# Attention transposes moved ahead of the second FF matmul, the small FF groups moved by one cycle, and the first image's bias additions and the second image's norm chain moved

**Chip, cores, metric.** One core of one Trainium2 chip. The metric is device time in microseconds, as the median of several executions; all executions told here are in the fast state. A ratio is the mean time of one kernel's fast runs over the mean time of the other's fast runs of the same rounds, so it is not quite the ratio of the medians quoted beside it. The experiments ran on three chips; each ratio is against the kernel before on the same chip.

## The reference, cut to what matters

Two residual layers on an NHWC tensor of 32 images, 56 x 56 pixels, 128 channels, float32:

```python
x = x + window_attention(group_norm(x))       # 7x7 windows shifted by 3, 4 heads, relative bias, mask
x = x + feed_forward(fourier(group_norm(x)))  # 128 -> 512 -> relu -> 128

def fourier(x):   # once along the width, once along the height, summed
    modes = dct(x, norm='ortho')[..., :32]
    mixed = einsum('bixy,ioy->boxy', modes, w)
    return idct(pad_to_56(mixed), norm='ortho')
```

## The kernel before

The kernel is a software pipeline over rows of windows (8 rows an image, 256 in all), one "cycle" a row. In a cycle, TensorE works for several rows and images at once: q and k of this row, scores, v, values (attention times v) and projection of the row before the last, and the Fourier and feed-forward (FF) work of the two images before. The order on the four compute engines is set by hand; the transfers that SyncE issues (SP in the traces) are not in that set, and the toolchain places them. In the traces PE is TensorE, DVE VectorE, ACT ScalarE, POOL GpSimd. An eviction is the copy of a finished matmul result out of the accumulator bank that TensorE wrote it to.

```python
FF_GROUPS = (HB, HB, HB, HB, 320, 256, HB)   # HB = 512 tokens
FF_AT = (7, 8, 9, 10, 12, 13, 14)            # cycles of an image; none at 11
...
def full_first(cycle, norm):                 # full-array work, head of the cycle
    im, i = row(cycle - 2)
    if im:
        attn_transpose(im, i, cycle - 2)     # "aT": attention transposed for the values
    ...
    attn_qk(im, i, False)
    ... load_modes(im, width, g)             # "zT": mixed modes back from DRAM
    ... ff_in(im, FF_AT.index(c))
...                                          # half_columns, quarters (scores, modes_back), eighths (values)
def full_last(cycle, norm):                  # full-array work, tail of the cycle
    next(norm)
    if row(cycle - 2)[0]:
        last_out(cycle)                      # second FF matmul
    next_image(cycle)                        # 7 transposes of the next image
    if row(cycle)[0]:
        attn_exp(cycle)
    attn_project(im, j)                      # needs "oT", the evicted values
...
with tc.manual_schedule(engines={ET.PE, ET.Activation, ET.DVE, ET.Pool}):
```

## Time and profile before

| | us |
|---|---|
| time, median of 3 | 3668.28 (3667.28 to 3670.64) |
| span of the profiled run | 3669.3 |
| TensorE busy | 3603.8 (98%) |
| start: constants and first rows, to the first image's statistics | 106.1 |
| first image (no FF work yet) | 93.4 |
| 29 steady images | 3254.6, about 112 each |
| last but one image, and the end | 101.8 and 113.4 |

How to read it: an engine with 98% busy time can only be helped where it stands still or is started late, so the waits of TensorE (PE) are the list to work from. The prediction below shows the rows it used. It did not use one kind of row of the same list, those with the releaser "issue", which means that the profile shows nothing that PE was waiting for. Between 216 and 3540 us, these are three of the five largest rows of the kernel before (line, releaser, total, times, longest):

```profile
PE pc L633 <- issue: 3.8, 6, 1.0
...
PE pa L524 <- ACT oT L515: 1.0, 2, 0.7
PE pa L482 <- issue: 0.8, 2, 0.4
```

L633 is the Fourier transform, L482 the values: both are long runs of small matmuls. They matter later. (Line numbers move between kernels: in the changed kernel these two are L637 and L486.)

### The profile page before, as it was taken

The page shows a single profiled execution, that of the slowest core. Times are in us where ns is not written, and L with a number is a line of the kernel's source. Part 1 is how long each engine was busy: PE and PEld are TensorE (multiplying, and loading weights), DVE is VectorE, ACT ScalarE, POOL GpSimd, SP SyncE. Part 2 cuts the span into 40 slices and gives each one's busy share as a digit, 9 for nine tenths or more (in the row PEclk, how much of TensorE's full clock was granted, in tenths as well). Part 3 has the DMA queues.
Part 4 walks back from the last instruction along what each step waited for, and adds up shares of the span by engine and source line. Part 5 has one row for each costly group of instructions (what it writes and reads, how often), then busy time and mean ns, then how long its engine had stood idle before and what let it go on. Part 6 is the DMA issues. An engine that isn't in the chain of part 4 may idle for free.

```text
span 3669.3 us, 139900 instructions
## 1 busy us (share of the span) xinstructions
PE 3603.8 (98%) x61184; PEld 2938.0 (80%) x61184; DVE 2222.3 (61%) x4741; ACT 2152.8 (59%) x4043; POOL 1371.9 (37%) x1421
## 2 busy tenths in 40 slices
PE   7899999999999999999999999999999999999998
PEld 5687888888888888888888888878888888888786
DVE  7766666656666566666566665666656666656641
ACT  5565556655565656566555666565665565665653
POOL 5433334333334333343333343333343333433321
PEclk9999999999999999999999999999999999999999
DMA  4334443433433334334434334443344343443333
GB/s 116 97 102 111 107 109 93 118 106 102 115 97 106 108 106 113 105 98 118 106 101 117 97 108 107 109 111 99 103 110 110 102 115 98 111 108 106 96 108 90
DMA packets 687795, 388.93 MB, mean 106 GB/s; under 512 B 40495, under 2 KB 658128, under 8 KB 686928
## 3 DMA queue, kind: packets, MB, share of 16 engines
q1 hardware_dynamic: 686573, 379.65, 38.1%
q8 instruction: 482, 7.90, 0.9%
q14 instruction: 129, 1.06, 0.1%
q10 hardware_dynamic: 611, 0.32, 0.0%
HBM read 218.29 MB, written 161.48 MB: 103 GB/s over the span
## 4 chain that ended last, share of the span: by engine, by line
PE 91%; DVE 4%; ACT 2%; POOL 1%; issue 1%; DMA 0%; SPq 0%; POOLq 0%; DVEq 0%; ACTq 0%
PE pc L769 21%; PE pc L749 17%; PE pa L391 7%; PE pc L667 6%; PE pc L633 6%; PE pa L413 6%; PE pa L457 5%; PE pc L706 5%; PE pa L524 5%; PE pa L482 4%; PE pa L359 4%; PE pa L366 4%; PE pa L262 2%; POOL a L432 1%; DVE a L421 1%; DVE mx L431 1%
## 5 line engine op out<-in xcount | busy, mean ns | idle before, releaser
L769 PE MATMUL pc<-wff,hid 128*128 128x128 f32 (+1 forms) x6400 | 779.1, 279 | 1.0 <-ACT hid L757 0.9
L446 POOL TENSOR_TENSOR a<-a,rs 128x784 f32<-128x784 f32 x256 | 389.6, 1522 | 993.0 <-DVE rs L445 869.7
L769 PEld LDWEIGHTS pc<-wff,hid 128*128 128x128 f32 (+1 forms) x6400 | 731.1, 189 | 24.0 <-issue 2.9
L749 PE MATMUL pc<-xf,wff 128*128 128x512 f32 (+2 forms) x1792 | 710.9, 539 | 0.9 <-DVE xf L717 0.6
L757 ACT ACTIVATE hid<-pc,b1sb 128x512 f32<-128x512 f32 (+2 forms) x896 | 536.4, 635 | 93.0 <-PE pc L749 89.4
L749 PEld LDWEIGHTS pc<-xf,wff 128*128 128x128 f32 x1792 | 339.5, 190 | 310.3 <-issue 229.4
L432 POOL TENSOR_TENSOR a<-a,mx 128x784 f32<-128x784 f32 x256 | 388.8, 1519 | 456.9 <-DVE mx L431 448.0
L781 DVE TENSOR_TENSOR res<-pc,res 128x512 f32<-128x512 f32 (+3 forms) x259 | 144.1, 568 | 607.7 <-issue 293.9
L289 POOL TENSOR_TENSOR xl<-xl,bproj 112x512 f32<-112x512 f32 (+1 forms) x256 | 286.0, 1138 | 347.3 <-PE pa L262 338.8
L421 DVE TENSOR_TENSOR a<-pa,bm 128x392 f32<-128x392 f32 x512 | 259.7, 550 | 203.2 <-PE pa L413 203.1
L438 ACT ACTIVATE a<-a 128x784 f32<-128x784 f32 x256 | 225.0, 879 | 222.3 <-POOL a L432 221.9
L379 DVE TENSOR_SCALAR k<-pa,heads,bqkv 128x392 f32<-128x392 f32 x246 | 168.6, 685 | 288.0 <-ACT k L371 288.0
L465 ACT COPY aT<-pa 113x452 f32<-113x452 f32 x256 | 137.5, 537 | 303.0 <-PE pa L457 298.7
L398 ACT COPY v<-pa 128x512 f32<-128x512 f32 x256 | 152.5, 596 | 268.4 <-PE pa L391 268.3
L739 POOL TENSOR_TENSOR res<-res,b2sb 128x512 f32<-128x512 f32 (+2 forms) x256 | 263.7, 1035 | 98.5 <-DMA res<-scr 88.3
L413 PEld LDWEIGHTS pa<-k,q 64*64 64x64 f32 x8192 | 183.6, 132 | 137.7 <-DVE rs L445 67.5
L513 DVE TENSOR_SCALAR oT<-pa,bqkv 128x98 f32<-128x98 f32 (+2 forms) x768 | 170.6, 278 | 200.0 <-PE pa L482 200.0
L391 PE MATMUL pa<-wn,xw 128*64 128x128 f32 x4096 | 282.5, 280 | 5.4 <-DVE a L421 2.9
L391 PEld LDWEIGHTS pa<-wn,xw 128*64 128x64 f32 x4096 | 220.3, 137 | 55.5 <-issue 16.4
L524 PE MATMUL pa<-wproj,oT 128*112 128x128 f32 x1792 | 241.0, 274 | 12.6 <-DVE oT L513 7.2
L431 DVE TENSOR_REDUCE mx<-a 128x16 f32<-128x784 f32 x256 | 247.3, 966 | 5.5
L443 DVE TENSOR_REDUCE sm<-a 128x16 f32<-128x784 f32 x256 | 245.7, 960 | 5.0 <-ACT a L438 5.0
(91 smaller groups left out, 5899.7 us busy)
## 6 DMA issues: line engine op xcount, KB each, us to landing
zscr<-z SPq DMA_DIRECT2D x512, 112.0 KB
htok<-scr SPq DMA_DIRECT2D x256, 196.0 KB
zT<-zscr SPq DMA_DIRECT2D x192, 256.0 KB
res<-scr SPq DMA_DIRECT2D x160, 256.0 KB
out_dram<-res SPq DMA_DIRECT2D x128, 256.0 KB
scr<-xl SPq DMA_DIRECT2D x128, 224.0 KB
xl<-in_x_dram SPq DMA_DIRECT2D x32, 784.0 KB
xl<-in_x_dram SPq DMA_DIRECT2D x32, 672.0 KB
```

The lines of the kernel that those rows point to most:

```text
L289: nc.gpsimd.tensor_tensor(piece, piece, bproj.unsqueeze(1).to_broadcast([TC, e - a, C]), ALU.add)
L391: nc.tensor.matmul(pv[hs, j * C : (j + 1) * C], lhsT=im.xw[i][:, w * WT : w * WT + JP], rhs=im.w[:, 2 * C : 3 * C], start=True, stop=True,)
L413: nc.tensor.matmul(ps[hp][HALVES[e], pr * 2 * WT : (pr + 1) * 2 * WT], lhsT=q[cs, w * WT : w * WT + JP], rhs=k_sb[cs, :, w], start=True, s ...
L421: nc.vector.tensor_tensor(a[:, 2 * hp : 2 * hp + 2, :, 0:WT].rearrange("p u w j -> p w u j"), ps[hp][:, :RT].rearrange("p (w u j) -> p w u ...
L431: nc.vector.tensor_reduce(mx, a3, axis=AX.X, op=ALU.max)
L432: nc.gpsimd.tensor_tensor(a3, a3, mx.unsqueeze(2).to_broadcast([P, 2 * NWR, WT]), ALU.subtract)
L446: nc.gpsimd.tensor_tensor(a3, a3, rs.unsqueeze(2).to_broadcast([P, 2 * NWR, WT]), ALU.mult)
L524: nc.tensor.matmul(pp[:TC, (n - n0) * C : (n - n0 + 1) * C], lhsT=oT[:, (n - base) * TC : (n - base + 1) * TC], rhs=wproj, start=True, sto ...
L739: nc.gpsimd.tensor_tensor(res[:m, c0:c1], res[:m, c0:c1], b2sb[:m].unsqueeze(1).to_broadcast([m, c1 - c0, C]), ALU.add,)
L749: nc.tensor.matmul(ph[:, :n], lhsT=wff1[:, f * P : (f + 1) * P], rhs=xff[:, t0 : t0 + n], start=True, stop=True,)
L757: nc.scalar.activation(hf[:, :n], ph[:, :n], AF.Relu, bias=b1sb[:, f : f + 1])
L769: nc.tensor.matmul(pf[:m, c * C : (c + 1) * C], lhsT=im.hid[f][:, c * P : c * P + m], rhs=wff2[:, f], start=(f == 0), stop=(f == NF - 1),)
```

## The change

Its intent: the transposes of the attention for the values of the next cycle move from the head of a cycle to the tail of the one before, ahead of the second FF matmul and the projection, so that they are work that waits for nothing while the projection's input gets ready. The small FF groups move by one cycle. At the start, the bias additions leave the first image's norm chain, and the second image's norm chain moves behind the values.

```diff
-FF_GROUPS = (HB, HB, HB, HB, 320, 256, HB)
+FF_GROUPS = (HB, HB, HB, HB, HB, 320, 256)
...
 def full_first(cycle, norm):
-        im, i = row(cycle - 2)
-        if im:
-            attn_transpose(im, i, cycle - 2)
...
+    def transpose_next(cycle):
+        im, i = row(cycle - 1)
+        if im:
+            attn_transpose(im, i, cycle - 1)
...
     def full_last(cycle, norm):
+        transpose_next(cycle)
         next(norm)
-        if row(cycle - 2)[0]:
+        im, j = row(cycle - 2)
+        if im:
             last_out(cycle)
+            attn_project(im, j)
         next_image(cycle)
         if row(cycle)[0]:
             attn_exp(cycle)
-        im, j = row(cycle - 2)
-        if im:
-            attn_project(im, j)
...
 def first_rows(cycle, norm):                  # the first ten rows
             attn_exp(cycle - 1)
-        next(norm)
...
             attn_values(im2, i2, cycle - 2)
+        next(norm)
...
+        if cycle < NWR // 2:
+            image_bias(im, 2 * cycle)         # taken out of image_groups for image 0
```

More of the change, by code (lines that the diff above doesn't have):

```diff
@@ L247, in image_begin @@
         im.x = xls.pop(b) if b in xls else load_image(b)
-        im.xw = {}
+        im.xw, im.aT = {}, {}
         im.st = small.tile([P, NWR, 6], F32, tag="st0", name="st0", bufs=2)
@@ L284, in image_groups, with image_bias @@
             nc.vector.bn_stats(im.st[:, i + k], xw)
+        if im.b:
+            image_bias(im, i)
+    def image_bias(im, i):
         n0, n1 = WS * i // 2, WS * (i + 2) // 2
@@ L452, in attn_transpose @@
         a = a_sb[r % 3]
-        im.aT = []
+        im.aT[i] = []
         for hf in range(2):
@@ L467, in attn_transpose @@
                 nc.vector.tensor_copy(aT[:PW, :, :PW], src)
-            im.aT.append(aT)
+            im.aT[i].append(aT)
     def attn_values(im, i, r):
@@ L484, in attn_values @@
                             lhsT=v[ks, 2 * f + e, h * HD : (h + 1) * HD],
-                            rhs=im.aT[f][ks, h, e * JP : e * JP + WT],
+                            rhs=im.aT[i][f][ks, h, e * JP : e * JP + WT],
                             start=True,
@@ L950, in first_rows @@
             attn_project(im2, i2)
+            transpose_next(cycle)
         next(norm)
```

## The prediction

> **What bounds the kernel now.** I read the page first, then the matmul engine's waits, then the timeline of one image in the middle, then the chain of waits at the start and the timeline at the end.
>
> ```profile
> span 3669.3 us, 139900 instructions
> PE 3603.8 (98%) x61184; PEld 2938.0 (80%) x61184; DVE 2222.3 (61%) x4741; ACT 2152.8 (59%) x4043; POOL 1371.9 (37%) x1421
> ...
> PE 91%; DVE 4%; ACT 2%; POOL 1%; issue 1%; DMA 0%; SPq 0%; POOLq 0%; DVEq 0%; ACTq 0%
> ```
>
> TensorE is busy for all but 65 us. The change neither adds nor removes a matmul, so it can only win back time in which PE stands still, or is started late. The waits of PE over the whole run, largest first:
>
> ```profile
> PE pa L348 <- DVE nb L342: 8.6, 2, 7.4
> PE pa L524 <- DVE oT L513: 7.2, 5, 2.3
> PE pa L262 <- DMA xl<-in_x_dram: 6.5, 1, 6.5
> ...
> PE pa L413 <- DVE k L379: 3.5, 14, 1.5
> ...
> PE pa L391 <- ACT aT L465: 2.4, 4, 0.7
> ```
>
> Asked by stretch, between 216 and 3540 us only about 9 us of named waits remain; 6.2 us of the L524 row, all of the L391 row and 1.5 us of the L413 row lie between 100 and 216 us, the first image. So I split the run into start, first image, steady images and end.
>
> **One steady image.** It takes about 112 us. The part with something in it is the one cycle without a feed-forward (FF) group and the cycle after it, here on PE (start, duration, what, count, wait before it):
>
> ```profile
> 1819.06 0.81 PE L482 MATMUL pa<-aT,v 49*32 49x49 f32 x64
> 1819.80 0.99 PE L262 MATMUL pa<-ident_x,xl 112*128 112x112 f32 x7
> 1820.93 1.10 PE L524 MATMUL pa<-wproj,oT 128*112 128x128 f32 x8
> 1821.86 0.96 PE L457 MATMUL pa<-ident,a 113*113 113x113 f32 x8
> 1822.66 0.84 PE L359 MATMUL pa<-xw,wn 128*128 128x392 f32 x2
> 1823.33 0.84 PE L366 MATMUL pa<-xw,wn 128*128 128x392 f32 x2
> 1824.01 2.32 PE L749 MATMUL pc<-xf,wff 128*128 128x320 f32 x8
> 1826.48 0.90 PE L413 MATMUL pa<-k,q 64*64 64x98 f32 x32 [0.15 <-DVE k L379]
> ```
>
> Starts matter more than durations here. L262 to L524 takes 1.13 us where elsewhere in the image (1810.12 to 1810.84) it takes 0.72: 0.41 us lost, because the projection needs oT, which DVE has only at 1820.78. L749 to L413 takes 2.47 us; eight matmuls of 320 columns should take 2.25 us (the 512 group takes 3.53, the 256 group 1.82, the least that I see for 320 in another image is 2.25): 0.22 us lost on k. Its cause is in the chain of waits of the same stretch:
>
> ```profile
> 1820.78 0.89 DVE mx L431
> ...
> 1821.80 1.53 POOL a L432
> ...
> 1823.36 0.88 ACT a L438
> 1824.23 0.41 ACT aT L465
> 1824.65 0.49 ACT q L362
> 1825.13 0.58 ACT k L371
> ...
> 1825.74 0.70 DVE k L379
> ```
>
> The copy of the transposed attention (aT, L465) stands in ScalarE's queue behind the exponential (L438) and ahead of q and k.
>
> [...] inside a full-array block the first load of a group starts 0.11 us before its matmul, but the first load after the 49x32 tiles (L482) starts with it, whoever comes next; so moving the transposes in front of L769 only passes that 0.1 us from one to the other. [...] PEclk here 0.53:
>
> ```profile
> 79.00:90.00 11.00, 9.32 (x110) 7.35 (x89) 5.75 (x15) 5.17 (x12) 3.03 (x2) 0.53 0.05 14
> ```
>
> [...] L323 has a median of 191 ns and a maximum of 1274 ns, the latter in image 0's norm chain beside the bias additions (L289).
>
> **The change, part by part.**
>
> Transposes first. L457 (8 x 99 ns = 0.79 us) moves from behind the projection to just behind L482. In cycles with an FF group nothing waits there now (L769 takes 3.68 us and hides oT), so the sum is unchanged. In the cycle without one, L457 (0.79 plus 0.09 for the exposed load) takes L262's place in front of the projection; oT still comes at 1820.78, L524 still starts at 1820.93, and L262 (0.72) instead of L457 (0.79) follows it: 0.07 us saved an image, not 0.41. The aT copy leaves the chain shown above, about 0.4 us there. At the image's end L348, one column wide, is now followed by L359 instead of L457; of the 0.16 us by which L457 and L359 run long behind it now (0.895 + 0.735 against 0.793 + 0.673) I expect 0.05 back.
>
> FF groups. The last three cycles of an image hold 512, 320, 256 instead of 320, 256, 512. The cycle with the k wait gets 512, 1.06 us longer than 320, so that wait goes: 0.22 plus 0.04 at L366 and L706. The price: 256 now falls on the first row of an image, which has three small ScalarE operations more. There L359 starts at 1850.02 and k is ready at 1853.35; with 256 the scores would want it at 1850.02 + 0.74 + 0.66 + 1.82 = 1853.24, so a wait of about 0.15 appears. For the 320 cycle, image copies and the exponential now stand before q: L359 + 1.6 for q, + 3.5 for k, against a demand at + 3.58: 0 to 0.1 of wait. Sum of a steady image: 0.07 + 0.05 + 0.26 - 0.15 - 0.05 = 0.18 us, times 30 = 5 us.
>
> First image (100 to 216 us; no FF work before the last of its cycles, so the chain of waits sets the pace). The waits of L391 for aT go, 4 x 0.6 = 2.4. The projection's waits of 1.06, 1.78 and 2.26 us for oT are partly filled by the transposes, 0.8 each, but where k follows as the next wait (L413, 1.5 us) only the 0.5 of the aT copy stays: 0.4 + 0.5 + 1.0, say 2. Perhaps the half-clock window at 178 to 182 us goes, 1 on average. Sum 5 us.
>
> Start. The bias additions (8 x 1.1 us on GpSimd) leave image 0's norm chain, which should fall from 5.2 us (13.85 to 19.04) to image 1's 2.7. But the start does not hang on it. From the chain of waits:
>
> ```profile
> 14.71 0.89 SPq L161
> ...
> 19.77 1.93 DMA rpb<-rpb_cols
> 21.88 2.82 DVE bm L182 x16
> ...
> 27.62 1.05 DVE a L421 x2
> ```
>
> The bias table's small DMAs and 32 DVE additions hold the first softmax to 27.62 us, and each of the next rows follows in a loop of 5.8 us through DVE, GpSimd and ScalarE (L421 at 27.62, 33.43, 39.19). L348 will start 2.5 us earlier, and the gain ends at L421. The additions (2.2 us a row) fit between subtraction and division: exponential 0.9, sum 1.0, reciprocal 0.3. Gain 0.
>
> Image 1's norm chain, moved from before to after the values: the 2.20 us stall of L413 on L532 (at 77.93) goes. But the chain now starts near 79.8 on DVE, takes 2.7, then GpSimd 0.6, the row's sums 1.1 and nb, so L348 comes at about 83.9 where it now comes at 83.29: the stall moves to L348. Loss 0.5, with the half-clock stretch about as long.
>
> End. In the last image one wait for zT of 2.64 us (L706 at 3594.95) stands behind the 320 group; 512 gives it 1.8 us more cover, and about 1 us comes back two cycles later, where 256 covers less. The last group has two chunks instead of four, so two DMA issues of 0.4 us fewer before the last one (now at 3666.25), and 0.2 less of waiting for the last hidden tile. Gain 2 us.
>
> Total: 5 + 5 + 0 - 0.5 + 2 = 11.5; with the half-hidden waits of an image (the mean period is 0.35 us over the shortest) a little may come on top. From 3668.3 I predict 3656 us.
>
> **Rivals.** (1) The stalls only move: k at the 256 cycle, k and the hidden evictions at the 320 cycle, since image copies are now squeezed between projection and q. For it: the margin of 3.5 against 3.58 is thin[...]. Each 0.1 us an image costs 3 us; two of 0.2 would eat the gain: 3668. (2) The projection gains its whole 0.41 us an image, and ScalarE being freer removes the scattered excess too: 0.4 x 30 + 5 + 10 + 2 = some 25 to 30 us, 3640. Against it: oT's time is set by DVE after the scores, not by PE's order. (3) The start shortens by the norm chain's 2.5 us and the half-clock stretch vanishes, 5 more: 3648. Against it: the chain through L161 and L182. (4) The additions in rows 0 to 3 delay GpSimd's subtraction and lengthen the 5.8 us loop: up to 4 us worse, 3660. For it: row 3 has 4.5 us of additions.
>
> **Range.** 80% from 3643 to 3665; 2% is 73 us, more than all idle time of PE, so within 2% is nearly certain: 0.98, faster 0.015, slower 0.005.
>
> **What would show it.** Right: L457 directly behind L482; L524 in the cycle without FF still starting 1.1 us after L482's successor; no k wait behind 512, a new one of 0.1 to 0.2 us behind 256; no L391 wait for aT; L348 of image 0 near 17.6 us but L421 still at 27.6; the L413 stall near 78 us gone and L348 waiting some 5 us instead; steady images about 0.2 us shorter. Wrong: image periods shorter by 0.5 us or more, the first L421 earlier than 27 us, or new PE waits on ScalarE behind the 320 group.

## The result

The changed kernel took 3665.49 us (median of 6, 3661.83 to 3667.58), the kernel before 3668.3 (6 runs) beside it: ratio 0.999, 95% interval 0.9977 to 1.0003. Measured once more on another chip: 3671.46 (13 runs) against 3674.1, ratio 0.9986 (0.9978 to 0.9995). The first interval alone still allows no gain at all; with both, the change is worth some 3 to 5 us, and the predicted 12 are not there.

The page of the changed kernel: span and busy time, then the queue that brings instructions, then the chain that ended last.

```profile
span 3661.5 us, 139922 instructions
...
PE 3603.5 (98%) x61184; PEld 2940.9 (80%) x61184; DVE 2224.1 (61%) x4739; ACT 2123.3 (58%) x4043; POOL 1372.0 (37%) x1421
...
q8 instruction: 482, 7.90, 0.9%
...
PE 94%; ACT 2%; DVE 2%; DMA 1%; issue 1%; POOL 0%; SPq 0%; ACTq 0%; POOLq 0%; DVEq 0%
```

PE's share of the chain rose from 91 to 94% and DVE's fell from 4 to 2%: named waits did go away. To see where the time went, I cut both traces at the first statistics matmul of each image (L575 before, L579 after), for the first pair of profiles and for a second pair taken on one other chip:

| stretch, us | before | after | before, again | after, again | predicted difference |
|---|---|---|---|---|---|
| start, to the first statistics | 106.1 | 105.0 | 103.6 | 105.5 | 0 (norm chain of image 1: +0.5) |
| first image | 93.4 | 92.0 | 91.6 | 92.9 | -5 |
| 29 steady images | 3254.6 | 3254.9 | 3260.0 | 3260.7 | -5 |
| last but one | 101.8 | 101.5 | 101.7 | 101.4 | in the row above |
| end | 113.4 | 108.1 | 111.3 | 108.2 | -2 |

Only the end got shorter in both pairs. The steady images did not, and this is the puzzle. For each block of matmuls (a run of one line on PE) I took the time from its start to the start of the next block, its median over the 29 images, and the sum of what the images lie above that median, the "scattered excess":

| 29 steady images | before | after | before, again | after, again |
|---|---|---|---|---|
| median image (sum of the block medians), us | 111.933 | 111.701 | 111.927 | 111.701 |
| scattered excess, us in all | 8.5 | 15.6 | 14.1 | 21.4 |

The median image is 0.23 us shorter, as predicted (0.18). The scatter ate it: 7.0 us more on one chip, 7.3 on the other, against 29 x 0.23 = 6.7 us gained. (The second chip adds some 5.7 us to both kernels, so an excess is only to be compared on one chip.) Each column is a single execution, and the spans of the pairs differ by -7.8 and +0.6 us where the medians of all runs beside them differ by -2.8 and -3.0 (6 and 13 runs of each kernel); so the 7 us are known to a few us only.

The cycle without FF group of the changed kernel, to be held against the same cycle in the prediction (start, duration, what):

```profile
1816.15 0.91 PE L417 MATMUL pa<-k,q 64*64 64x98 f32 x32
1816.99 0.81 PE L486 MATMUL pa<-aT,v 49*32 49x49 f32 x64
1817.80 1.03 PE L461 MATMUL pa<-ident,a 113*113 113x113 f32 x8
1818.85 1.10 PE L528 MATMUL pa<-wproj,oT 128*112 128x128 f32 x8
1819.79 0.88 PE L262 MATMUL pa<-ident_x,xl 112*128 112x112 f32 x7
...
1821.83 3.60 PE L753 MATMUL pc<-xf,wff 128*128 128x512 f32 x8
1825.36 0.91 PE L417 MATMUL pa<-k,q 64*64 64x98 f32 x32
```

The transposes (L461) stand behind the values (L486), the projection (L528) follows 1.05 us later where 0.88 is the median in most other cycles, and the scores after the 512 group come 3.53 us after its start without a wait.

The waits of PE in the steady part, in the first image, and the stall in image 1's norm:

```profile
PE pa L486 <- issue: 6.5, 13, 1.0
PE pa L528 <- ACT oT L519: 2.2, 3, 1.1
PE pc L637 <- issue: 0.7, 2, 0.5
```

```profile
PE pa L461 <- POOL a L450: 3.7, 3, 2.4
...
PE pa L417 <- DVE k L383: 1.1, 2, 0.8
PE pa L528 <- DVE oT L517: 1.0, 1, 1.0
PE pa L461 <- POOL y L623: 0.5, 1, 0.5
```

```profile
76.69 1.09 PE L395 MATMUL pa<-wn,xw 128*64 128x128 f32 x16 [0.50 <-DVE a L425]
82.36 0.56 PE L352 MATMUL pa<-nb,wqkv 128*128 128x1 f32 x2 [4.57 <-DVE nb L346]
```

First fence: of what is left in the steady part the largest row is one of "issue", in the values. Second: in the first image the waits for aT are gone and the one for oT fell from 6.2 to 1.0 us, but the transposes, which now come almost a cycle earlier, wait for GpSimd's division (L450), 3.7 us, and once more 0.5 us that the profile puts down to another GpSimd instruction (L623). Third: the stall in the start moved to L352, as predicted.

### The profile page after: what moved, and what is told of

Read it like the earlier page. It is cut to its first block, busy times and chain, and to the rows that moved or that the text cites. A ratio compares the mean times of both kernels' runs of the same rounds, so it can differ in the third digit from the quotient of the medians.

```text
span 3661.5 us, 139922 instructions
## 1 busy us (share of the span) xinstructions
PE 3603.5 (98%) x61184; PEld 2940.9 (80%) x61184; DVE 2224.1 (61%) x4739; ACT 2123.3 (58%) x4043; POOL 1372.0 (37%) x1421
## 4 chain that ended last, share of the span: by engine, by line
PE 94%; ACT 2%; DVE 2%; DMA 1%; issue 1%; POOL 0%; SPq 0%; ACTq 0%; POOLq 0%; DVEq 0%
PE pc L773 19%; PE pc L753 17%; PE pa L395 7%; PE pa L461 7%; PE pc L671 6%; PE pc L637 6%; PE pa L528 6%; PE pa L417 6%; PE pa L486 5%; PE pa L363 5%; PE pc L710 5%; PE pa L370 4%; PE pa L262 2%; ACT k L375 1%; DVE k L383 1%
## 5 line engine op out<-in xcount | busy, mean ns | idle before, releaser
L773 PE MATMUL pc<-wff,hid 128*128 128x128 f32 x6400 | 760.4, 276 | 0.9 <-ACT hid L761 0.8
L773 PEld LDWEIGHTS pc<-wff,hid 128*128 128x128 f32 x6400 | 732.3, 190 | 9.4 <-issue 2.4
L450 POOL TENSOR_TENSOR a<-a,rs 128x784 f32<-128x784 f32 x256 | 389.5, 1522 | 874.0 <-DVE rs L449 869.5
L425 DVE TENSOR_TENSOR a<-pa,bm 128x392 f32<-128x392 f32 x512 | 259.5, 549 | 178.8 <-PE pa L417 178.7
L280 ACT COPY xw<-pa 128x392 f32<-128x392 f32 x128 | 62.3, 486 | 396.1 <-PE pa L262 396.1
L417 PEld LDWEIGHTS pa<-k,q 64*64 64x64 f32 x8192 | 183.4, 132 | 133.6 <-DVE rs L449 45.5
L395 PE MATMUL pa<-wn,xw 128*64 128x128 f32 x4096 | 282.7, 281 | 3.9 <-DVE a L425 3.9
L366 ACT ACTIVATE q<-pa,bqkv 128x392 f32<-128x392 f32 x256 | 150.5, 588 | 218.8 <-PE pa L363 217.3
L461 PE MATMUL pa<-ident,a 113*113 113x113 f32 x2048 | 267.3, 273 | 5.3 <-POOL a L450 4.4
L395 PEld LDWEIGHTS pa<-wn,xw 128*64 128x64 f32 x4096 | 220.4, 137 | 53.8 <-ACT xw L275 16.2
```

What stands on the lines that cost most here:

```text
L395: nc.tensor.matmul(pv[hs, j * C : (j + 1) * C], lhsT=im.xw[i][:, w * WT : w * WT + JP], rhs=im.w[:, 2 * C : 3 * C], start=True, stop=True,)
L417: nc.tensor.matmul(ps[hp][HALVES[e], pr * 2 * WT : (pr + 1) * 2 * WT], lhsT=q[cs, w * WT : w * WT + JP], rhs=k_sb[cs, :, w], start=True, s ...
L425: nc.vector.tensor_tensor(a[:, 2 * hp : 2 * hp + 2, :, 0:WT].rearrange("p u w j -> p w u j"), ps[hp][:, :RT].rearrange("p (w u j) -> p w u ...
L450: nc.gpsimd.tensor_tensor(a3, a3, rs.unsqueeze(2).to_broadcast([P, 2 * NWR, WT]), ALU.mult)
L461: nc.tensor.transpose(pt[:PW, h * P : h * P + PW], a[:PW, h, 2 * hf : 2 * hf + 2].rearrange("p w j -> p (w j)")[:, :PW], ident[:PW, :PW],)
L773: nc.tensor.matmul(pf[:m, c * C : (c + 1) * C], lhsT=im.hid[f][:, c * P : c * P + m], rhs=wff2[:, f], start=(f == 0), stop=(f == NF - 1),)
```

## The experiments

There were eleven runs, two of them repeats of the two kernels, all with correct results. I began with one part of the change at a time. Where an expectation says "fetch", it supposes that the stalls of PE by "issue" are waits for its instructions (page and trace of the changed kernel: 482 instruction packets of 16.4 KB beside 123,463 PE instructions); what the traces show of this stands under "The scatter".

### Each part alone

**Transposes only**: the changed kernel with the FF groups, bias additions and norm chain of the kernel before.

```diff
-FF_GROUPS = (HB, HB, HB, HB, HB, 320, 256)
+FF_GROUPS = (HB, HB, HB, HB, 320, 256, HB)
(and bias additions and norm chain as before)
```

> The kernel before with the attention's transposes first, and nothing else of the change. Theory A (the parts win what the median image shows, and lose it to new waits and to the fetch of TensorE's instructions): the wait for k of 0.22 us behind the 320 group goes, since the copy of the transposed attention no longer stands before q and k on ScalarE, but one of about 0.3 us appears behind the 256 group of the next cycle; the median image, 111.93 us before, loses 0.05 to 0.15; the whole about 3 us shorter, 3665. Rival B (the order of the transposes is worth nothing, all comes from the FF groups and the two ends): 3668, the median image unchanged within 0.03.

Measured: 3686.87 us (5 runs) beside 3674.05, ratio 1.0035 (1.0023 to 1.0048). It is slower than both kernels, which I had not expected.

**FF groups only**: the kernel before with one line changed.

```diff
-FF_GROUPS = (HB, HB, HB, HB, 320, 256, HB)
+FF_GROUPS = (HB, HB, HB, HB, HB, 320, 256)
```

> The kernel before with the FF groups 512 x5, 320, 256 and nothing else. Theory A: the k wait behind the former 320 cycle goes (0.26 us an image with what hangs on it), one of 0.15 us comes in the first row's cycle, where 256 now stands; the median image 0.1 us shorter; fetch stalls in the values' block of that cycle, 3 us over the run, which the kernel before does not have; the end 4 us shorter. Whole 3664, 4 us shorter. Rival B: the end alone, 4 us, with no new stalls; then the median image gives 3 us more, 3661.

Measured: 3690.75 us (5 runs), ratio 1.0044 (1.0031 to 1.0056). Slower again, where 4 us less was expected.

**Start only**: the kernel before with the bias additions and norm chain of the changed one.

> The kernel before with the bias additions and the norm chain of the start moved, and nothing else. Theory A: the first softmax stays held by the bias table, the wait for the norm moves from the scores to L348's place; the first statistics matmul 1 us earlier (106.1 to 105.0), whole 3667. Rival: the half-clock stretch near 80 us shrinks and later waits with it, 3 to 5 us shorter, 3664.

Measured: 3675.13 us (13 runs), ratio 1.0002 (0.9994 to 1.001). As expected in this: L352 comes at 18.74 us and nothing later comes earlier. In the changed kernel the start looks like this:

```profile
17.62 0.56 PE L352 MATMUL pa<-nb,wqkv 128*128 128x1 f32 x2 [4.72 <-DVE nb L346]
...
21.82 5.70 DVE L182 TENSOR_TENSOR bm<-rpb,mask 49x98 f32<-49x98 f32 x32 [3.45 <-DMA rpb<-rpb_cols]
...
27.56 1.04 DVE L425 TENSOR_TENSOR a<-pa,bm 128x392 f32<-128x392 f32 x2
```

L352 is 2.5 us earlier than in the kernel before, the bias table (L182) is not, and the first softmax (L425) starts at 27.56 instead of 27.62.

So two parts of the change, each harmful alone (+13 and +17 us), make a small gain together. The waits of PE over the whole run show what went wrong in each; first transposes only, then FF groups only:

```profile
PE pc L705 <- DMA zT<-zscr: 7.7, 15, 1.1
PE pa L412 <- DVE k L378: 7.4, 32, 0.8
```

```profile
PE pc L706 <- DMA zT<-zscr: 14.7, 27, 1.4
```

L705 and L706 are the same matmul line, the mode block. In both kernels it waits for its input zT, which comes back from DRAM, and neither part of the change names that transfer. In the cycle that has the 256 group, FF groups only shows this on SyncE and PE:

```profile
1747.53 0.93 SPq L801 DMA_DIRECT2D out_dram<-res  x2
...
1748.69 0.42 SPq L688 DMA_DIRECT2D zT<-zscr  x1
1749.21 0.44 SPq L538 DMA_DIRECT2D scr<-xl  x1
1749.70 0.48 SPq L688 DMA_DIRECT2D zT<-zscr  x1
...
1753.70 1.00 PE L706 MATMUL pc<-idctw,zT 64*64 64x112 f32 x32 [0.50 <-DMA zT<-zscr]
...
1754.95 1.00 PE L706 MATMUL pc<-idctw,zT 64*64 64x112 f32 x32 [0.26 <-DMA zT<-zscr]
```

and the changed kernel, in the same cycle, this:

```profile
1735.92 0.93 SPq L692 DMA_DIRECT2D zT<-zscr  x2
1737.16 1.13 PE L528 MATMUL pa<-wproj,oT 128*112 128x128 f32 x8
1737.78 0.96 SPq L805 DMA_DIRECT2D out_dram<-res  x2
...
1739.67 1.89 PE L753 MATMUL pc<-xf,wff 128*128 128x256 f32 x8
...
1742.38 1.71 PE L710 MATMUL pc<-idctw,zT 64*64 64x112 f32 x64
```

In FF groups only, both zT loads stand in SyncE's queue behind the two output stores of the 320 group, which wait for that group's result (over the run, L801 waits 1083.7 us for res in 183 waits), and the second load also behind the store of the projected image (L538). It takes some 5 us from issue to use (1748.69 to 1753.70), and the 256 group gives less cover than the 512 group had given. In the changed kernel the toolchain put both loads ahead of the stores: 6.5 us from issue to need. In transposes only it is the cycle behind the one without FF group: the image store slipped in between the two loads.

I tested this by setting the place of the loads.

### The loads' place in the queue

**FF groups only, loads early**, and **transposes only, loads early**: the loads of one cycle are written at the tail of the cycle before.

```diff
 def full_first(cycle, norm):
     for im, c in fourier(cycle):
-        for width, g in back_groups(c):
-            load_modes(im, width, g)
+        if c != 6:                       # 4 in "transposes only"
+            for width, g in back_groups(c):
+                load_modes(im, width, g)
 def full_last(cycle, norm):
     next(norm)
+    for f, c in fourier(cycle + 1):
+        if c == 6:
+            for width, g in back_groups(c):
+                load_modes(f, width, g)
     ... last_out(cycle)
```

> The kernel of 'FF groups only' with one thing more: the mode loads (zT) of the first row's cycle stand in the program one step earlier, ahead of the stores of the previous FF group, so that on the transfer queue they come before the last store of the 320 group instead of behind both stores. Theory (place in the transfer queue): the waits of the mode matmuls for zT, 14.7 us in 27 images, fall under 2 us; that block goes from 2.18 back to about 1.65 us, the median steady image from 112.45 to about 111.9, and the time from 1.0044 of the kernel before to about 1.000 (some 15 us less than 'FF groups only'). The wait on k behind the 256 group (0.16 us an image) stays, and the stalls of PE that no wait explains stay too. Rival (the transfer itself is slower, or the 256 group simply covers too little): the zT waits stay above 10 us and the ratio stays near 1.004.

> The kernel of 'transposes only' with the mode loads (zT) of the cycle behind the one without FF group one step earlier in the program, which puts the image store between the two loads behind both, as in the kernel before. Theory (place in the transfer queue): the second load goes out 0.5 to 1 us earlier; the mode block falls from 2.01 to between 1.66 and 1.80 us, the zT waits from 7.7 to under 3 us, and the time from 1.0035 to about 1.001 of the kernel before. The k waits behind the 256 group (7.4 us) and the unexplained stalls (11 us in the values block) stay, so it does not get under the kernel before. Rival (the loads wait for the z stores, wherever they stand in the queue): block still at 1.9 or more, ratio still 1.003.

Measured: FF groups only goes from 1.0044 to 1.0015 (1.0007 to 1.0023), 3681.75 us; transposes only from 1.0035 to 1.0006 (0.9997 to 1.0014), 3676.98 us. In both, the mode block is back at 1.641 us (from 2.18 and 2.01), and of the zT waits 2.2 us are left in transposes only (7.7 before) and none of 0.4 us or more in FF groups only; transposes only, loads early:

```profile
PE pc L705 <- DMA zT<-zscr: 2.2, 4, 1.1
```

So the place in the queue is what made the loads late: shown, as nothing else was moved in the program. The second expectation held (9 us expected, 10.7 came). The first was only two thirds right: I expected 15 us and 10.7 came. The median image of FF groups only fell from 112.45 to 112.29, not to 111.9, because another wait stood behind the one removed. FF groups only, loads early:

```profile
1750.91 2.21 DVE L717 TENSOR_TENSOR xf<-pc,xf 128x448 f32<-128x448 f32 x4
1752.54 2.05 PE L769 MATMUL pc<-wff,hid 128*128 128x128 f32 x16
1753.04 0.96 DVE L431 TENSOR_REDUCE mx<-a 128x16 f32<-128x784 f32 x1
1753.91 0.66 DVE L513 TENSOR_SCALAR oT<-pa,bqkv 128x98 f32<-128x98 f32 x3
...
1754.72 0.88 PE L524 MATMUL pa<-wproj,oT 128*112 128x128 f32 x6
```

The second FF matmul of the 256 group lasts 2.05 us, and the projection (L524) needs oT, which DVE finishes at 1754.57 because it comes behind the evictions of the mode block (L717) and the row maximum of the softmax (L431). PE loses 0.30 us from L769's start to L524's and 0.06 behind it, per image. In the changed kernel the transposes stand in front of L773, 0.88 us of work that hides just this. That is the coupling of the two parts: the 256 group at the first row needs the transposes in front of the projection. The transposes alone (cycle of 256 unchanged) make k late there: the group takes 2.09 us to the scores instead of 1.82, the 7.4 us of k waits above. Perhaps it is because they took their work away from between projection and scores; this is read from the order and was not tested. In the cycle behind it the transposes also wait for the division (they start 0.92 us after the values instead of 0.74). I did not find out why the toolchain orders the queue as it does.

### The scatter: whose is it?

The kernel before and the changed kernel once more, unchanged, on one chip.

> The kernel before, unchanged, profiled once more beside the changed kernel on one chip. The question is whether the 8.5 us of scattered excess over the median steady image (29 images) in its first profile belongs to the kernel or to the chip and the run: the kernel with only the start changed has the same steady instructions and showed 14.2 us on another chip. If it is the chip or the run: excess 12 to 16 us here, and the changed kernel has as much. If it is the kernel: 7 to 10 us again, and the changed kernel 14 to 17. The median steady image stays at 111.93 us.

> The changed kernel, unchanged. Median steady image 111.70 us again; scattered excess 14 to 17 us over 29 images, with PE's unexplained stalls in the values block of the width cycle and of the image's first row, in the same images as before (1 to 5, 14 to 19, 28 and 29; 10 to 14 and 24 to 28), if they belong to the position in PE's instruction stream. Time against the kernel before: 0.999 as in the first comparison if the excess belongs to the kernel; 0.996 to 0.997 (11 to 14 us less) if both kernels have the same excess on one chip.

The result is in the tables above: the scatter belongs to both. Each kernel has 5.6 to 5.8 us more on this chip than on the first, and the changed kernel has some 7 us more than the kernel before on either. Neither of my two alternatives was it. The waits by "issue" in the steady part, kernel before and changed kernel, on this chip:

```profile
PE pc L633 <- issue: 4.7, 5, 1.3
...
PE pa L482 <- issue: 1.8, 4, 0.6
```

```profile
PE pa L486 <- issue: 11.2, 18, 1.5
...
PE pc L637 <- issue: 1.1, 2, 0.7
```

The stalls sit in the same two blocks, which stand back to back in the cycle of the width transform (112 transform matmuls, then 64 value matmuls), and in the values block of an image's first row. By excess over the median, over 29 images: transform 6.6 us before and 2.6 after, values behind it 2.1 and 10.6, values of the first row 0.3 and 3.9.

The experiments above, cut in the same way, tell which part moves which. In the values behind the transform, the five kernels with moved transposes that keep these two blocks together (changed, transposes only with loads late and early, small groups early, split mixes) have 6.5 to 11.1 us, the four without moved transposes 1.5 to 4.4; in the transform it is the other way round, 0.1 to 2.6 and 4.9 to 7.1. The sum of the two blocks hardly tells them apart (6.8 to 13.1 and 7.0 to 11.5): the transposes move these stalls more than they add to them. The values of the first row have 3.6 to 5.5 us where the 256 group stands in their cycle (changed kernel; FF groups only with loads early), 0.2 to 1.4 where it does not. FF groups only with its late loads has the 256 group there too, but 0.8: there PE waits for zT just before.

What are they? In the traces each of them begins at a PE instruction (weight loads, matmuls and semaphore instructions counted together) whose number is 193 to 195 more than a multiple of 256 (193 throughout in the changed kernel): all 187 stalls by "issue" in the steady parts of the thirteen traces of this case do. The page's instruction queue moved 482 packets in 7.90 MB, 16.4 KB each, and PE has 123,463 instructions: one packet for each 256. (The place in each 256 at which the stalls begin is called the boundary below, and the start of a packet of that queue a fetch.) That these stalls are waits of PE for its next instructions is inferred from this count and from the times of the packets. In the 20 stalls of the changed kernel on the second chip, the last fetch had started 2.2 to 2.9 us before PE went on, when PE stood only 85 to 223 instructions before the boundary; in its 15 stalls on the first chip it was 2.3 to 3.4 us and 119 to 217 instructions. Boundaries in the first half of the transform, which do not stall, have their fetch some 6 to 12 us ahead. The two blocks together are 352 instructions in 4.1 us, the values alone 128 in 0.74.

An image of the changed kernel has 3858 PE instructions, 15 x 256 + 18, so a boundary that falls in the values block moves by 18 instructions, 9 matmuls, from image to image. That can be seen in the changed kernel's timeline (second chip), in images 2, 3 and 4: what is left of the 64 matmuls behind the stall is 30, 39, 48.

```profile
317.19 0.40 PE L486 MATMUL pa<-aT,v 49*32 49x49 f32 x30 [0.51 <-issue]
...
430.73 0.59 PE L486 MATMUL pa<-aT,v 49*32 49x49 f32 x39 [1.54 <-issue]
...
543.20 0.66 PE L486 MATMUL pa<-aT,v 49*32 49x49 f32 x48 [0.38 <-issue]
```

If that is the cause, 36 instructions more at the start must make every stall come two images earlier.

**Phase shift**: the changed kernel with nine tiny matmuls ahead of the bias matmul of image 0.

```diff
         pb = attn_bank()
+        for _ in range(9 if im.b == 0 else 0):
+            nc.tensor.matmul(pb[:32, 1:2], lhsT=wqkv[:, :32], rhs=wqkv[:, :1], start=True, stop=True)
         nc.tensor.matmul(pb[:, 0:1], lhsT=wqkv[:, 2 * C :], rhs=nb, start=True, stop=True)
```

> The changed kernel with nine tiny matmuls more (36 PE instructions, under 2 us, in the start's stall) ahead of everything steady. Theory (the stalls come where PE's instruction count crosses a multiple of 256): 36 instructions are what the count drifts in two images (3858 is 15 x 256 + 18), so each stall appears two images earlier than in the changed kernel, at the same place: the values block of the width cycle in images 1 to 3, 12 to 17, 26 and 27; the values block of the first row in 8 to 12 and 22 to 26. The time stays within 3 us of the changed kernel. Rival (the stalls come from memory traffic or from something tied to the image): same images as in the changed kernel, or no order in them.

Measured, in images 1, 2 and 3 of this kernel:

```profile
208.28 0.59 PE L488 MATMUL pa<-aT,v 49*32 49x49 f32 x39 [0.19 <-issue]
...
322.43 0.66 PE L488 MATMUL pa<-aT,v 49*32 49x49 f32 x48 [1.48 <-issue]
434.94 0.74 PE L488 MATMUL pa<-aT,v 49*32 49x49 f32 x57 [0.27 <-issue]
```

39, 48, 57: what images 3 and 4 had is now in 1 and 2. Over all images, the stalls in the values behind the transform lie in images 1 to 3, 11 to 15, 17 and 26 to 29 (changed kernel: 1 to 5, 13 to 15, 17 to 19, 28 and 29), those of the first row in 8, 9, 11, 12, 22 and 24 to 26 (changed kernel: 10 to 14, 24 to 26 and 28). The shift by two is there, with a few images at the edges that I had not named. The rival that memory traffic or the image sets the place of the stalls falls; that traffic sets their size was not tested. The place of a stall is set by the instruction count; its size is not, it differs for the same position (1.54 us in image 3, 0.19 in image 1 of the shifted kernel). The time is 3671.9 us (12 runs), within a microsecond of the changed kernel's 3671.46 in the median; by the ratios of means (0.9999 and 0.9986, with overlapping intervals) it is 4.8 us longer, so the 3 us that I had allowed are not clearly met. The profiled run was the longest of them (3680.25, in the fast state), and its scattered excess is 26.9 us.

### Ways to more

**Small groups early**: the changed kernel with the small FF groups where more full-array work is, so that no cycle with a tight k has a short one.

```diff
-FF_GROUPS = (HB, HB, HB, HB, HB, 320, 256)
+FF_GROUPS = (256, HB, 320, HB, HB, HB, HB)
```

> The changed kernel with the small FF groups moved to cycles in which nothing stands before q on ScalarE: 256, 512, 320, 512 x4. Theory A: no wait for k anywhere in a steady image, so the median image 0.15 us shorter than the changed kernel's 111.70, and the fetch stalls in the values' block of the first row's cycle (3.4 us in the changed kernel's trace) go[...]; last group of 512 costs 1 us at the end: 3658. Rival B (fetch stalls are chance and stay at 15 us in all): 3663.

Measured: 3654.39 us (5 runs), ratio 0.9947 (0.9933 to 0.996): it beats both kernels, by about twice the 10 us that I had expected against the kernel before. The median image is 111.505 us, 0.20 below the changed kernel (0.16 of it is the k wait behind the 256 group, which is gone), and the stalls in the first row's values fall to 1.0 us (3.6 and 3.9 in the two profiles of the changed kernel). So the 256 group in the first row's cycle, predicted to cost a k wait of 0.15 us, seems to cost in a second way: where it is gone, most of the stalls behind it are gone as well. Whether the k wait or the shorter group brings them is not shown (this kernel ran on another chip than those two profiles, and other groups moved too, so the size is not sure either). The stalls behind the width transform stay:

```profile
PE pa L486 <- issue: 6.1, 12, 0.9
```

**Split mixes**: small groups early, and in the cycle without FF group the scores go between the second and third of four mixing groups.

```diff
+    def split_three(cycle):      # in place of half_columns and quarters there
+        attn_v(im, i, cycle)
+        mix(f, False, 0); mix(f, False, 1)
+        attn_scores(im, i, cycle)
+        mix(f, False, 2); mix(f, False, 3)
```

> The kernel with the small FF groups early (0.9947), and in the cycle without FF group the scores moved between the second and third of the four mixing groups, so that the projection no longer waits for the normalised output oT behind the evictions of the scores. If the projection's 0.4 us an image was lost because DVE gets to the scores too late: L482's successor to projection from 1.05 to about 0.72, the median image from 111.5 to 111.2, some 9 us in all: 0.9947 goes to about 0.992. Rival: the scores come 1.4 us earlier than now, q and k are not evicted yet, and the wait moves to the scores: within 3 us of 0.9947.

Measured: 3657.65 us (5 runs), ratio 0.995 (0.9938 to 0.9963): no gain. The values go from 0.818 to 0.738 us and the way from the transposes to the projection from 1.050 to 0.953, so 0.18 us of the projection's delay is won; but the mixes take 1.847 + 1.898 instead of 3.593, 0.15 us more as two blocks than as one; why, no run tests. The number is that of my rival (within 3 us of 0.9947), but not for its reason: the scores (L417) do not wait in the steady part.

**Values before columns**: split mixes, and the 64 value matmuls ahead of v and the 112 transform matmuls.

```diff
-                    half_columns(cycle)
-                    eighths(cycle)
+                    if 0 in [c for _, c in fourier(cycle)]:
+                        eighths(cycle)
+                        half_columns(cycle)
```

> As the split mixes, and in the cycle with the width transform the 64 small value matmuls go ahead of the 112 transform matmuls instead of behind them. Theory (PE's instructions arrive in blocks of 256[...]): the unexplained stalls in this place, 6 to 11 us in the other kernels, fall under 3 us, because full-array work stands between the two; 4 to 7 us less than the split mixes, about 0.990. Rival (the stalls come wherever a block ends, whatever stands there): the stalls move to other blocks and the time equals that of the split mixes within 2 us.

Measured: 3734.6 us (4 runs), ratio 1.0159, 77 us slower than split mixes. The stalls in question did go, from 5.9 us in split mixes to 0.8:

```profile
PE pa L395 <- DVE a L425: 53.4, 29, 1.8
...
PE pa L486 <- issue: 0.8, 1, 0.8
```

but v (L395) now stands 1.84 us in each image until DVE has added the bias to the scores (L425), probably because it takes the accumulator bank that they leave; the transform block takes 4.41 us instead of 3.37 as well, which I did not follow up. So this run does not tell whether the other work in between made the stalls vanish or the new wait did, and not that either is worth anything.

## Why the prediction was right or wrong

That the time would stay within 2% was right, and so was the reason, that PE has only 65 us to lose. The time was 3665.5 us against 3656, 0.5 us above the range by the median (by the ratio, 0.999 x 3668.3 = 3664.6, just inside it). By its steps:

- **Steady image, -0.18 us: right**, -0.23 measured, and so are nearly all of its terms. The cycle without FF group gained 0.08 (0.07 predicted: 0.818 + 1.049 + 0.935 + 0.715 against 0.738 + 1.130 + 0.935 + 0.793) and the projection still starts late there; L352's followers gained 0.09 (0.05); the k wait behind 512 is gone; the 256 group takes 1.98 us instead of 1.82 (0.15 predicted as a wait, 0.16 measured); the 320 group has no wait (0 to 0.1 predicted).
- **"A little may come on top" from the half-hidden waits: the step that failed.** It took the scatter (0.35 us an image; 112.23 less 111.93, 0.30, by the cut used here) for something that the change could only lessen. It is mostly stalls of PE at one place in every 256 of its instructions (all 187 in the thirteen traces), by inference waits for the instructions themselves; it was in the list of waits that I read ("issue", 3.8 us in the transform), and I left these rows out because they had no releaser. It rose by 7.0 and 7.3 us in two pairs of single executions, of which some 5 and 7 lie in the transform and the values, and cancelled 29 x 0.23. The part that is alike in both pairs is that of the first row's values, 3.4 and 3.6 us. Shown: that the place of these stalls hangs on the instruction count; that with the transposes moved they go from the transform into the values; and that those of the first row come with the 256 group in its cycle, late loads apart. Open: why they go there when the transposes follow those blocks instead of leading the cycle.
- **First image, -5 us: mis-sized.** Measured -1.4 in one pair and +1.3 in the other. The waits for aT and most of those for oT went, as the step says; it missed that transposes moved ahead need the division earlier (3.7 + 0.5 us on GpSimd). The half-clock windows turned out against it too: the one at 178 to 182 us did go, as hoped (granted clock 0.57 before, 1.00 after), but one came at 166 to 170 us (0.57), and between 100 and 216 us the mean granted clock fell from 0.97 to 0.96, in the second pair from 0.99 to 0.94. Why they fall where they do was not followed up.
- **Start, 0: right; image 1's norm, +0.5: right in kind.** L352 at 17.62 (17.6 predicted), L425 unmoved, the L413 stall gone and L352 of image 1 waiting 4.57 us; but it comes at 82.36 us, 0.9 earlier than before (83.29) and not 0.6 later, and 0.1 earlier in the second pair. The granted clock of 0.53 between 79 and 90 us in the kernel before follows a stall of 2.20 us, with PE busy for 1.80 of the 4 us from 75 to 79; what lowers the clock there, no run tests. The start differs by -1.1 and +1.9 in the two pairs, and start only is at 1.0002.
- **End, -2 us: too small**, -5.3 and -3.1. The zT wait fell from 2.6 to 0.4 us and did not come back two cycles later, as I had assumed for 1 us of it, and in the first pair a half-clock window near 3595 us is gone (granted clock from 3593 to 3597 us 0.76 before, 1.00 after).
- **Rivals.** The first (3668) comes nearest by its number, but not by its reason: no k or eviction wait ate the gain. The second (projection gains its whole 0.41 us) fell, and split mixes shows why it is hard: 0.18 us can be had, for 0.15. The third and fourth fell with start only.

What no rival had: the two parts depend on each other, through the transfer queue (shown by the two kernels with loads early) and through the cover of the projection.

## What to carry to other kernels

A wait without a releaser on the engine that sets the end is still a wait: find out what it repeats with (here every 256 instructions) before a rearrangement moves it. After any reordering, look also at the queues that nobody ordered by hand, because a load that slips behind a store can cost more than the change was to bring (here 14.7 us of waits for zT, against 12 us predicted). And try the parts of a change alone and in another mixture: here two of the three parts, each alone, were slower by 0.4%, and another order of the same group sizes took 0.5% off.
